# One of the seven products of a pair of score tiles, made as seven products of quarter size

## The chip, the cores and the metric

The kernel runs on one core of one Trainium2 chip. The metric is device time in microseconds (us) of that core, the median of several runs. Lower is better.

## The reference, cut to what matters

Two graph layers over 4096 nodes with 512 features each. Layer 0 adds `relu(adj @ signs)` to `x` and normalises. Layer 1 is masked attention, and the change lies in its scores `e = h @ h.T`:

```python
# layer 0
xw  = max(sign(x), 0) @ sign(weight).T
x   = layernorm(x + relu(adj @ xw))
# layer 1
h   = x @ edge_w                         # 4096 x 512, float32
e   = h @ h.T                            # 4096 x 4096 scores, float32
e   = where(adj > 0, e, -9e15)
att = softmax(x @ node_w, axis=0) * softmax(e, axis=1)
x   = layernorm(x + (adj * att) @ (x @ weight) + bias)
```

The scores are symmetric, so only one triangle of tiles is computed, and the mirrored tile is its transpose.

## The kernel before

`hT` holds `h` transposed: 128 partitions, four slices of the 512 features, 4096 nodes. The score matrix is cut into tiles of 512 x 512 (`W` = 512), numbered by row `A` and column `B`, 0 to 7. Single tiles are made by `Single` (line L706, a plain product). The others come in pairs: `Couple(A, B)` makes tile (A, B) and tile (A, B+1), 512 rows by 1024 columns, with Strassen's scheme in Winograd's form: the rows are halved (blocks `u` of 128 rows inside each half `q`), the features are halved, and the columns are halved, so that seven products of half size take the place of eight. `Couple.operands` builds the sums for this: four sums `t1` to `t4` of the column operand for each `B` (L747 to L750), and four sums `s1` to `s4` of the row operand for each couple (L764 to L767), all on VectorE (DVE).

`Couple.quad(q, between)` makes one half `q` of a couple. `multiply(bank, m)` (L779) issues product number `m`: two matmuls of 128 x 128 weights and 512 moving columns, because half the features are two slices. An fp32 matmul shows as two records in the trace, so one such product is four records. The order and what follows each product is:

- product 0 into bank `y`, copied to `c11` by ScalarE (ACT, L803); product 1 into bank `x`, added to `c11` by DVE (L806);
- product 5 added into `y`, copied to `c12` (L810); product 4 into `z`;
- product 6 added into `y`, copied to `c22` (L816), then `z` added to it by DVE (L817);
- product 3 added into `y`, copied to `c21` (L821); product 2 added into `z`, and `z` added to `c12` (L824). Then both strips of rows, (c11, c12) and (c21, c22), are complete: `written(0)` and `written(1)`.

A strip is half of a `lent` buffer (`free_h` holds 14 such halves). For every complete strip three kinds of work are queued: DVE masks it and takes the row minimum (L629, L630), after which ACT takes the exponential (L639); TensorE (PE) transposes it for the mirrored tiles (L668), and ACT copies the transposes out (L669), which then get their own L630 and L639; the GpSimd queue (POOL) stores it (L796), and the mirrored tiles too (L682). The masks come in by SyncE's queue (SP, L611, L614).

There are twelve couples in three runs: four for B = 4, six for B = 6, two for B = 2, with Single tiles before, between and after them. In a run, the quads of neighbouring couples are interleaved by hand as generators (`next(first)`, `next(second)`, `next(rest_)`), and `between()` counts the steps (`tick`) and lets queued work out. A scheduler then places the instructions of PE, DVE and ACT in this stage by when it expects them to be ready; each engine runs its list in order. From the aggregation stage on (L955 and after) the order is fixed by hand.

Of the kernel before, what the change touches and what calls it, by code (L numbers as in the profile page):

```python
# [11 lines left out]
F32 = mybir.dt.float32  # L12
# [6 lines left out]
P = 128  # L19
# [10 lines left out]
def kernel(  # L30
# [13 lines left out]
    nc = tc.nc  # L44
# [3 lines left out]
    W = 512  # L48
# [12 lines left out]
    ps_mm = ctx.enter_context(tc.tile_pool(name="ps_mm", bufs=6, space=bass.MemoryType.PSUM))  # L61
# [97 lines left out]
    with (  # L159
# [281 lines left out]
        l11, l12 = we_s[:, :HK, :HD], we_s[:, HK:, :HD]  # L441
        l21, l22 = we_s[:, :HK, HD:], we_s[:, HK:, HD:]
        s4, s1, s2, s3 = (lops[:, n] for n in range(4))
# [88 lines left out]
    free_h = deque(h for t in lent for h in t[1:])  # L532
# [195 lines left out]
                    stats.append((at_once, 0, store))  # L728

    class Couple:  # L730
        right = {}
        made = [0]

        def __init__(self, A, B):
# [6 lines left out]
        def operands(self):  # L741
            A, B, h = self.A, self.B, KD // 2
            if B not in Couple.right:
                r11, r12 = (hT[:, :h, ts(c, W)] for c in (B, B + 1))
                r21, r22 = (hT[:, h:, ts(c, W)] for c in (B, B + 1))
                t1, t2, t3, t4 = (lopp.tile([P, h, W], F32, name="right", tag="lop") for _ in range(4))
                nc.vector.tensor_sub(t1, r12, r11)  # L747
                nc.vector.tensor_sub(t2, r22, t1)
                nc.vector.tensor_sub(t3, r22, r12)
                nc.vector.tensor_sub(t4, r21, t2)  # L750
                Couple.right[B] = r11, r21, r22, t4, t1, t2, t3
            low, high = (hT[:, f : f + h, ts(A, W)].rearrange("p k (q u w) -> p k q u w", u=2, w=P) for f in (0, h))
            l11, l21 = (low[:, :, :, u, :] for u in range(2))
            l12, l22 = (high[:, :, :, u, :] for u in range(2))
            Couple.made[0] += 1
            self.sums = None
            if Couple.made[0] % 2:
                s2, s1, s3, s4 = (rows.tile([P, h, 2, P], F32, name="left", tag="rows") for _ in range(4))
            else:
                self.sums = Uses(1)  # L760
                s2, s1, s3, s4 = (
                    self.sums.buf[:, n, :].rearrange("p (k q w) -> p k q w", k=h, w=P) for n in range(4)
                )
            nc.vector.tensor_add(s1, l21, l22)  # L764
            nc.vector.tensor_sub(s2, s1, l11)
            nc.vector.tensor_sub(s3, l11, l21)
            nc.vector.tensor_sub(s4, l12, s2)  # L767
            self.left = l11, l12, s4, l22, s1, s2, s3

        def quad(self, q, between):  # L770

            left, right = self.left, Couple.right[self.B]
            x, y, z = (ps_mm.tile([P, W], F32, name="seven", tag="mm") for _ in range(3))
            strips = [Uses(4, free_h) for _ in range(2)]
            (c11, c12), (c21, c22) = ((s.buf[:, 0, :], s.buf[:, 1, :]) for s in strips)

            def multiply(ps, m, first=False):
                for k in range(KD // 2):
                    nc.tensor.matmul(  # L779
                        ps,  # L780
                        left[m][:, k, q, :],
                        right[m][:, k, :],
                        start=(first and k == 0),
                        stop=(k == KD // 2 - 1),
                        skip_group_check=not first,
                    )

            def written(u):
                s, i = strips[u], 2 * q + u
                here = self.here[i]  # L790
                stats.append((here.ready, 1, lambda: here.row(i, s, s.buf.rearrange("p c w -> p (c w)"))))
                for n, m in enumerate(self.mirrors):
                    turns.append((now[0] + 2, lambda m=m, n=n: m.turn(s, s.buf[:, n, :], i)))

                def store():
                    nc.gpsimd.dma_start(s_d[self.A][self.B // 2][:, i, :, :], s.buf)  # L796
                    s.used()

                stats.append((at_once, 0, store))


            multiply(y, 0, True)
            nc.scalar.copy(c11, y)  # L803
            between()
            multiply(x, 1, True)
            nc.vector.tensor_add(c11, c11, x)  # L806
            between()
            yield
            multiply(y, 5)
            nc.scalar.copy(c12, y)  # L810
            between()
            multiply(z, 4, True)
            between()
            yield
            multiply(y, 6)
            nc.scalar.copy(c22, y)  # L816
            nc.vector.tensor_add(c22, c22, z)  # L817
            between()
            yield
            multiply(y, 3)  # L820
            nc.scalar.copy(c21, y)  # L821
            between()
            multiply(z, 2)
            nc.vector.tensor_add(c12, c12, z)  # L824
            written(0)
            written(1)
            between()
            yield
# [52 lines left out]
    def spend(engine, cost, ready=0.0):  # L881
        clock[engine] = max(clock[engine], ready) + cost
        return clock[engine]
# [47 lines left out]
    class Aggregate:  # L931
# [143 lines left out]
        def second(self, m):  # L1075

            h, w = BG // 2, W // 2
            r = self.right(m)
            (r11, r12), (r21, r22) = [[r[:, k : k + h, c : c + w] for c in (0, w)] for k in (0, h)]
            t2, t3, t4 = (extra[0][:, n, :].rearrange("p (b w) -> p b w", w=w) for n in range(3))  # L1080
            self.halves = r11, r21, r22, t4, r12, t2, t3
            for o, a, b in ((t3, r22, r12), (r12, r12, r11), (t2, r22, r12), (t4, r21, t2)):
                nc.vector.tensor_sub(o, a, b)
                spend("dve", 0.69)
                yield
# [40 lines left out]
    written = deque()  # L1126
# [97 lines left out]
    inner, inner_next = deque(), deque()  # L1224
# [196 lines left out]
    def couples(B, *As):  # L1421
        return [Couple(A, B) for A in As]

    runs = [Single(2, 2), Single(2, 3), couples(4, 2, 3, 0, 1)]
    runs += [Single(4, 4), Single(4, 5), couples(6, 2, 3, 0, 1, 4, 5)]
    runs += [Single(3, 3), couples(2, 0, 1)]
    tail = len(runs)
    runs += [Single(0, 0), Single(0, 1), Single(1, 1), Single(6, 6), Single(6, 7), Single(7, 7), Single(5, 5)]
    masks = deque(r for u in runs for c in (u if isinstance(u, list) else [u]) for r in c.masks)
# [2 lines left out]
    def between():  # L1432
        tick()
        soon[0] = max(1, 2 - sum(m.t is not None for m in final))
        while masks and len(free_h) > 2 and masks_h[0] < 8 and masks[0].unit <= unit[0] + 1:
            masks.popleft().load()
        for _ in range(2):
            if closing[0] and len(early_) > 1 and (len(early_) > 10 or now[0] % 2) and early_[0][0]():
                early_.popleft()[1]()
            if len(early_) < 10:  # L1440
                break
# [10 lines left out]
    for n, u in enumerate(runs):  # L1452
        unit[0] = n
        closing[0] = n >= tail
        if isinstance(u, Single):
            final = []
            u.main(between)
            for later in runs[n + 1 : n + 3]:
                if isinstance(later, list) and later[0].left is None:
                    later[0].operands()  # L1460
            continue
        final = u[-1].mirrors
        quads = [[c.quad(q, between) for q in range(2)] for c in u]
        for k, c in enumerate(u):
            first, second = quads[k]
            rest_ = quads[k - 1][1] if k else None
            next(first)
            if rest_:
                next(rest_)
            next(first)  # L1470
            if rest_:
                next(rest_)
                if u[k - 1].sums:
                    u[k - 1].sums.used()
            next(first)
            next(second)
            if k + 1 < len(u):
                u[k + 1].operands()
            next(first)
            next(second)  # L1480
        next(rest_ := quads[-1][1])
        next(rest_)
        if u[-1].sums:
            u[-1].sums.used()
# [13 lines left out]
    r11, r12, r21, r22 = (w1_s[:, k : k + 2, c : c + HD] for k in (0, 2) for c in (0, HD))  # L1498
    t2, t3, t4 = (take(free_e).rearrange("p (k o) -> p k o", o=HD) for _ in range(3))
# [5 lines left out]
    with tc.manual_schedule(engines=order_):  # L1505
        for n, u in enumerate(blocks):
# [5 lines left out]
            first = deque()  # L1512
# [60 lines left out]
            if u.r == HG - 1 and nxt:  # L1573
                todo.extend(Todo(lambda g=u.g, n=n: join(g, n, nc.vector)) for n in range(7))
                second, other = (Finish(u.g, half) for half in (1, 0))
# [49 lines left out]
```

## Time and profile before

| | us |
|---|---|
| median of 3 runs | 1921.03 (1920.61 to 1921.36) |
| the profiled execution's own time | 1922.03 |
| its span in the trace | 1920.3 |
| PE busy (share of the span) | 1904.1 (99%) |
| DVE busy | 1437.1 (75%) |
| ACT busy | 1023.4 (53%) |
| POOL busy | 310.6 (16%) |
| the couples run in the trace from | 629 to 995, with Single tiles at 740 to 765 and 930 to 940 |

In the groups of the profile a row reads: line, engine, operation, what it writes and reads, shapes and count, then the busy time, the mean duration of one instruction in ns, and the idle time of the engine just ahead of them with what ended it. The durations of matmuls overlap, so that the distance between two starts is shorter than the duration. PEld is the load of weights, which runs beside the matmuls.

### The profile page before, as it was taken

The page shows a single profiled execution, that of the slowest core. Times are in us where ns is not written, and L with a number is a line of the kernel's source. Part 1 is how long each engine was busy: PE and PEld are TensorE (multiplying, and loading weights), DVE is VectorE, ACT ScalarE, POOL GpSimd, SP SyncE. Part 2 cuts the span into 40 slices and gives each one's busy share as a digit, 9 for nine tenths or more (in the row PEclk, how much of TensorE's full clock was granted, in tenths as well). Part 3 has the DMA queues.
Part 4 walks back from the last instruction along what each step waited for, and adds up shares of the span by engine and source line. Part 5 has one row for each costly group of instructions (what it writes and reads, how often), then busy time and mean ns, then how long its engine had stood idle before and what let it go on. Part 6 is the DMA issues. An engine that isn't in the chain of part 4 may idle for free.

```text
span 1920.3 us, 20431 instructions
## 1 busy us (share of the span) xinstructions
PE 1904.1 (99%) x6816; PEld 1220.4 (64%) x6816; DVE 1437.1 (75%) x2113; ACT 1023.4 (53%) x1647; POOL 310.6 (16%) x449
## 2 busy tenths in 40 slices
PE   8999999999999999999999999999999999999998
PEld 6888888888644445444555556666666666656646
DVE  6777677776875467576754877898879988898947
ACT  5433333333212468566767666656676567657731
POOL 0123132231421011111110111111111111110100
PEclk9999999999999999999999999999999999999999
DMA  8889898898585478477874888787777877787731
GB/s 307 288 327 354 318 333 322 326 356 317 177 300 199 153 280 321 178 255 276 306 282 156 309 291 299 285 292 287 266 282 279 298 277 276 264 308 250 285 117 55
DMA packets 143913, 520.93 MB, mean 271 GB/s; under 512 B 15040, under 2 KB 15040, under 8 KB 136128
## 3 DMA queue, kind: packets, MB, share of 16 engines
q1 hardware_dynamic: 64368, 235.43, 35.9%
q0 software_dynamic: 67632, 248.54, 34.2%
q10 hardware_dynamic: 11808, 35.66, 5.0%
q8 instruction: 54, 0.88, 0.2%
q14 instruction: 51, 0.42, 0.1%
HBM read 397.93 MB, written 121.63 MB: 271 GB/s over the span
## 4 chain that ended last, share of the span: by engine, by line
PE 89%; DVE 6%; ACT 2%; DMA 1%; issue 1%; ACTq 0%; DVEq 0%
PE bank L1186 33%; PE seven L779 14%; PE acc L424 11%; PE acc L423 11%; PE pe L706 5%; PE seven L101 5%; PE po L1336 4%; PE pt L668 2%; DMA lent<-in_adj_t_dram 1%; DVE slot L955 1%; PE pt L383 1%; PE acc L236 1%; PE acc L235 1%; PE pw L213 1%; PE bank L1336 0%
## 5 line engine op out<-in xcount | busy, mean ns | idle before, releaser
L1186 PE MATMUL bank<-lent,lop 128*128 128x256 f32 (+1 forms) x1496 | 483.0, 473 | 0.1
L1186 PEld LDWEIGHTS bank<-lent,lop 128*128 128x128 f32 x1496 | 283.8, 190 | 166.9 <-issue 140.1
L423 PE MATMUL acc<-xw,hi 128*128 128x512 f32 x960 | 376.4, 392 | 0.0
L424 PE MATMUL acc<-xw,lo 128*128 128x512 f32 x960 | 374.2, 390 | 0.0
L1186 PE MATMUL bank<-slot,lop 128*128 128x512 f32 (+1 forms) x800 | 286.6, 503 | 2.6 <-DMA lop<-lop_d 1.3
L413 ACT CAST hi<-at 128x1024 fp32r<-128x1024 f32 x120 | 126.5, 1054 | 203.7 <-PE acc L423 151.0
L1186 PEld LDWEIGHTS bank<-slot,lop 128*128 128x128 f32 x800 | 151.4, 190 | 117.6 <-issue 102.5
L1197 ACT COPY over<-bank 128x512 f32<-128x512 f32 x200 | 116.2, 586 | 199.8 <-PE bank L1186 195.9
L424 PEld LDWEIGHTS acc<-xw,lo 128*128 128x128 f32 x960 | 180.3, 188 | 37.1 <-DVE lo L415 0.3
L423 PEld LDWEIGHTS acc<-xw,hi 128*128 128x128 f32 x960 | 180.2, 188 | 36.7
L415 DVE TENSOR_TENSOR lo<-at,hi 128x1024 fp32r<-128x1024 f32 x120 | 147.9, 1232 | 66.8 <-ACT hi L413 66.4
L706 PE MATMUL pe<-hT 128*128 128x512 f32 (+3 forms) x384 | 132.1, 486 | 0.0
L639 ACT ACTIVATE line<-line,nmax_c 128x512 f32<-128x512 f32 x160 | 114.8, 725 | 22.6 <-DVE nmax_c L630 22.3
L630 DVE CUSTOM_DVE_ANT_0 line<-lent,slot 128x512 f32<-128x512 bf16 x140 | 90.7, 689 | 47.6 <-ACT slot L716 26.7
L1348 DVE SCALAR_TENSOR_TENSOR xb<-po,f,xb 128x256 f32<-128x256 f32 x84 | 40.2, 480 | 74.7 <-PE po L1336 70.5
L706 PEld LDWEIGHTS pe<-hT 128*128 128x128 f32 x384 | 64.6, 191 | 41.4 <-issue 33.8
L779 PE MATMUL seven<-hT 128*128 128x512 f32 x192 | 89.8, 593 | 0.0
L955 DVE CUSTOM_DVE_ANT_1 lent<-lent,line 128x2048 f32<-128x2048 f32 x39 | 88.7, 2283 | 0.0
L1159 ACT COPY bank<-over 128x512 f32<-128x512 f32 x144 | 86.7, 603 | 0.0
L668 PEld LDWEIGHTS pt<-ident,lent 128*128 128x128 f32 x418 | 52.3, 141 | 52.1 <-issue 38.5
L669 ACT COPY slot<-pt 128x512 f32<-128x512 f32 (+3 forms) x123 | 68.5, 560 | 23.2 <-PE pt L668 23.2
L958 ACT ACTIVATE lent<-lent 128x2048 f32<-128x2048 f32 x39 | 74.9, 1920 | 8.4 <-DVE lent L955 8.2
(270 smaller groups left out, 2947.0 us busy)
## 6 DMA issues: line engine op xcount, KB each, us to landing
lop<-lop_d SPq DMA_DIRECT2D x154, 512.0 KB, 4.7
at<-in_adj_t_dram SPq DMA_DIRECT2D x60, 1024.0 KB, 6.7
slot<-in_adj_t_dram POOLq DMA_DIRECT2D x39, 1024.0 KB, 8.0
lent<-s_d POOLq DMA_DIRECT2D x38, 1024.0 KB, 7.8
s_d<-slot POOLq DMA_DIRECT2D x30, 1024.0 KB, 7.0
lent<-in_adj_t_dram POOLq DMA_DIRECT2D x25, 1024.0 KB, 7.7
lent<-in_adj_dram SPq DMA_DIRECT2D x48, 512.0 KB, 5.0
s_d<-lent POOLq DMA_DIRECT2D x48, 512.0 KB, 4.1
```

The source lines that it names most:

```text
L101: nc.tensor.matmul(banks[bank][q], lop(m, q)[k], rop(m)[k], start=(first and k == 0), stop=(k == K - 1), skip_group_check=not first,)
L413: nc.scalar.copy(hi, aq)
L415: nc.vector.tensor_sub(lo, aq, hi.bitcast(F32))
L423: nc.tensor.matmul(acc, hi[:, c, :], xw[:, kb, :], start=(kb == 0), stop=False)
L424: nc.tensor.matmul(acc, lo[:, c, :], xw[:, kb, :], start=False, stop=(kb == NB - 1))
L639: nc.scalar.activation(line, line, AF.Exp, bias=nmax_c[:, b, c : c + 1], scale=-1.0, accum_out=sum_c[:, b, c : c + 1])
L668: nc.tensor.transpose(pt[:, j, :], src[:, ts(j, P)], ident)
L706: nc.tensor.matmul(pe[:, lo * P :], hT[:, k, ts(A * BG + i, P)], hT[:, k, (B * BG + lo) * P : (B + 1) * W], start=(k == 0), stop=(k == KD ...
L779: nc.tensor.matmul(ps, left[m][:, k, q, :], right[m][:, k, :], start=(first and k == 0), stop=(k == KD // 2 - 1), skip_group_check=not first,)
L955: pinned[0](nc.vector._custom_dve(TENSOR_ADD_SAT, out=q, in0=q, in1=m, s0=0.0, s1=-HUGE))
L1186: nc.tensor.matmul(ps, lop[:, k, :], rop[:, k, :], start=start, stop=(k == K - 1), skip_group_check=True)
L1197: nc.scalar.copy(self.to(), self.bank[:, : self.w])
```

## The change

Product 1 of both quads of a couple (features' second half of the upper blocks by the first column tile, second half of the features) is no longer issued by `quad`. Seen over both quads it is one product of 256 rows by 512 columns over 256 features, and it is cut once more by the same scheme: rows by quad, columns into two halves of 256 (`w`), features into two slices of 128. Seven products of one matmul each, with 256 moving columns, take the place of four matmuls with 512.

- `second_right` builds four sums of 128 x 256 for each `B`; `second_left` builds four sums of 128 x 128 for each couple. Each set lies in one half of a `lent` buffer, taken from `free_h`; the first is kept while its `B` lasts, the second until the couple is done.
- `second` issues the seven small products. They are named here by bank and number: u0, v1, u5, z4, u6, z2, u3, in this order. `u` is the left half of a bank `x`, `v` and `z` are the halves of a bank `y`. DVE adds the results to `c11` of the two quads: u to the left half after u0, to the right half after u5, z to the right half of the second quad's strip after z4, u to the same after u6, the whole bank `y` to the first quad's strip after z2, and u to the left half of the second quad's strip after u3. Products 5, 6 and 3 go on top of what stands in `u`, and 2 on top of `z`, once DVE has read it.
- A quad uses two banks instead of three. Its generator has one more stop, `c11` is complete later, and the first strip of the first quad is released from inside `second`. The twelve small stops are interleaved with the quads.

```diff
+                Couple.inner_right[B] = self.second_right(r21)
...
+            self.inner_left = self.second_left(l12)
+            self.rows11, self.written = [None] * 2, [None] * 2
+
+        def second_right(self, r):
+
+            w = W // 2
+            (r11, r12), (r21, r22) = ((r[:, k, :w], r[:, k, w:]) for k in range(2))
+            keep = Uses(sum(c.B == self.B for c in every), free_h)
+            t1, t2, t3, t4 = (keep.buf[:, n // 2, ts(n % 2, w)] for n in range(4))
+            nc.vector.tensor_sub(t1, r12, r11)
+            nc.vector.tensor_sub(t2, r22, t1)
+            nc.vector.tensor_sub(t3, r22, r12)
+            nc.vector.tensor_sub(t4, r21, t2)
+            return (r11, r21, r22, t4, t1, t2, t3), keep
+
+        def second_left(self, l):
+
+            (l11, l12), (l21, l22) = ([l[:, k, q, :] for k in range(2)] for q in range(2))
+            self.inner_sums = Uses(1, free_h)
+            s1, s2, s3, s4 = (self.inner_sums.buf[:, 0, ts(n, P)] for n in range(4))
+            nc.vector.tensor_add(s1, l21, l22)
+            nc.vector.tensor_sub(s2, s1, l11)
+            nc.vector.tensor_sub(s3, l11, l21)
+            nc.vector.tensor_sub(s4, l12, s2)
+            return l11, l12, s4, l22, s1, s2, s3
+
+        def second(self, between):
+
+            left, (right, keep) = self.inner_left, Couple.inner_right[self.B]
+            w = W // 2
+            c11, c12 = (self.rows11[0][:, c] for c in (slice(w), slice(w, W)))
+            x, y = (ps_mm.tile([P, W], F32, name="inner", tag="mm") for _ in range(2))
+            u, v, z = x[:, :w], y[:, :w], y[:, w:]
+
+            def multiply(ps, m, first=False):
+                nc.tensor.matmul(ps, left[m], right[m], start=first, stop=True, skip_group_check=not first)
+
+            multiply(u, 0, True)
+            nc.vector.tensor_add(c11, c11, u)
+            yield
+            multiply(v, 1, True)
+            multiply(u, 5)
+            nc.vector.tensor_add(c12, c12, u)
+            between()
+            yield
+            c21, c22 = (self.rows11[1][:, c] for c in (slice(w), slice(w, W)))
+            multiply(z, 4)
+            nc.vector.tensor_add(c22, c22, z)
+            yield
+            multiply(u, 6)
+            nc.vector.tensor_add(c22, c22, u)
+            multiply(z, 2)
+            nc.vector.tensor_add(self.rows11[0], self.rows11[0], y)
+            self.written[0]()
+            between()
+            yield
+            multiply(u, 3)
+            nc.vector.tensor_add(c21, c21, u)
+            self.inner_sums.used()
+            keep.used()
+            yield
 
         def quad(self, q, between):
 
-            x, y, z = (ps_mm.tile([P, W], F32, name="seven", tag="mm") for _ in range(3))
+            y, z = (ps_mm.tile([P, W], F32, name="seven", tag="mm") for _ in range(2))
...
+            self.rows11[q] = c11
...
             multiply(y, 0, True)
             nc.scalar.copy(c11, y)
             between()
-            multiply(x, 1, True)
-            nc.vector.tensor_add(c11, c11, x)
-            between()
+            self.written[q] = lambda: written(0)
             yield
             multiply(y, 5)
             nc.scalar.copy(c12, y)
             between()
+            if q:
+                yield
             multiply(z, 4, True)
...
+            if not q:
+                yield
             multiply(z, 2)
             nc.vector.tensor_add(c12, c12, z)
-            written(0)
+            if q:
+                written(0)
             written(1)
...
             next(first)
+            inner_ = inners[k]
+            next(inner_)
             next(second)
             if k + 1 < len(u):
                 u[k + 1].operands()
+            next(inner_)
             next(first)
+            next(inner_)
+            next(first)
+            next(inner_)
+            next(second)
+            next(inner_)
             next(second)
```

More of the change, by code (lines that the diff above doesn't have):

```diff
@@ L730 @@
     class Couple:
-        right = {}
+        right, inner_right = {}, {}
         made = [0]
@@ L1426 @@
     runs += [Single(3, 3), couples(2, 0, 1)]
+    every = [c for u in runs if isinstance(u, list) for c in u]
     tail = len(runs)
@@ L1463 @@
         quads = [[c.quad(q, between) for q in range(2)] for c in u]
+        inners = [c.second(between) for c in u]
         for k, c in enumerate(u):
```

## The prediction

> **What bounds the kernel now.** I read the page's busy shares first, then the busy time in windows of one couple each, then the groups with shapes kept apart, then the chain of waits from 600 us on. The page says that PE is the bound everywhere:
>
> ```profile
> PE 1904.1 (99%) x6816; PEld 1220.4 (64%) x6816; DVE 1437.1 (75%) x2113; ACT 1023.4 (53%) x1647; POOL 310.6 (16%) x449
> ```
>
> The windows (PE, PEld, DVE, ACT, POOL busy, clock, DMA share, GB/s) say how near the next engine is, couple by couple. A couple takes about 27.5 us, all of it PE; DVE has 10 us to spare in an early couple and 4.5 us in the last one of a run, where the column sums of the next `B` (L747 to L750) are built too:
>
> ```profile
> 656.50:684.00 27.50, 27.50 (x89) 13.77 (x88) 15.15 (x32) 16.48 (x36) 3.61 (x6) 1.00 0.58 211
> 711.50:739.00 27.50, 27.50 (x89) 13.66 (x89) 23.00 (x45) 20.38 (x43) 3.63 (x6) 1.00 0.80 283
> ```
>
> ```profile
> 904.60:932.00 27.40, 27.40 (x91) 13.75 (x91) 22.93 (x43) 18.72 (x40) 4.43 (x8) 1.00 0.84 303
> 939.70:967.00 27.30, 26.57 (x78) 12.48 (x77) 12.11 (x28) 17.47 (x43) 2.01 (x4) 1.00 0.69 257
> ```
>
> The groups give the durations:
>
> ```profile
> L1186 PE MATMUL bank<-lent,lop 128*128 128x256 f32 x840 | 196.3, 379 | 0.1
> L779 PE MATMUL seven<-hT 128*128 128x512 f32 x192 | 89.8, 593 | 0.0
> L779 PEld LDWEIGHTS seven<-hT 128*128 128x128 f32 x192 | 33.4, 190 | 26.8 <-issue 26.8
> L1348 DVE SCALAR_TENSOR_TENSOR xb<-po,f,xb 128x256 f32<-128x256 f32 x84 | 40.2, 480 | 74.7 <-PE po L1336 70.5 <-DMA lop<-lop_d 4.1
> L806 DVE TENSOR_TENSOR lent<-lent,seven 128x512 f32<-128x512 f32 x24 | 16.5, 687 | 48.0 <-PE seven L779 28.9 <-issue 19.1
> L1243 DVE TENSOR_TENSOR slot<-slot 128x256 f32<-128x256 f32 x16 | 6.7, 422 | 0.3
> ```
>
> The chain (start, us, engine, line) holds what the busy share hides. Nearly all of it is PE, but from 908 to 948 us it leaves PE: 39 us of DVE and ACT work end in a PE stall of 0.72 us at the start of the B = 2 run.
>
> ```profile
> 899.86 8.60 PE seven L779 x20
> ...
> 908.49 0.69 DVE lent L824
> ...
> 937.17 1.24 ACT lent L639 x2
> ...
> 945.22 2.11 ACT line L639 x6
> 947.33 0.48 ACT lent L810
> ...
> 947.86 10.57 PE seven L779 x24
> ```
>
> **What the Trainium skill says.** "TensorE: Matmul & The Clock Gate", section LDWEIGHTS, puts a weight load at columns/1.2 ns, 107 ns for 128; here it is 190 ns. That still fits under a 256-column record. "VectorE: DVE Perf Modes", section on the TRN2 errata, gives an fp32 add (N+151)/0.96 ns: 691 at 512 (here 687), 424 at 256 (here 422). No 128-column add shows here; the page prices it at 291 ns (estimate). "PSUM — Partial Sum Buffer", section Engine vs sequencer instructions, says that the queues of VectorE and ScalarE are strictly in order; the stall at 947 agrees, since the copy of `c12` (L810) stood behind a row of L639 exponentials. "DMA: Bandwidth & Descriptors", section Anatomy of one DMA, gives 2.0 us plus bytes at 436 GB/s, 3.2 us for a 512 KB store (estimate); L796 took 3.6 us (770 to 900 us) and 5.5 us (650 to 735 us).
>
> **PE's own work.** In unbroken stretches of the chain a 512-column record starts every 0.429 us (28 in 12.02 us); four 256-column ones (L1336 at 1303.9 us) take 0.87, 0.217 each. Per couple 8 records of 0.429 go (3.43 us) and 14 of 0.217 come (3.04 us): 0.39 us less, times 12 couples, **-4.7 us**. The load of 190 ns hides under 217.
>
> **DVE's own work, per couple:** two adds of 687 ns go; five of 256 columns (422) and one of 512 (687) come, with four row sums of 128 columns (291): +2.6 us. Per `B` four column sums of 422: +1.7 us. In all +36 us, beside PE's work where the spare of 10 us covers it. ACT, POOL and SP get no new work: the same copies, exponentials, stores and loads, only later or earlier. Buffers: 14 halves now also hold one for each `B` and up to two for couples. Counting the code's steps, masks are still loaded at least 8 steps ahead of their use (a couple has 14, so 2 us each), 16 us against a landing of 4 to 5: taken at nothing, up to 3 us if it is wrong.
>
> **The new waits, in a middle couple.** I follow the built order of the changed kernel with the durations above, from the end of the previous quad's product 6 (t = 0). PE: four transposes to 0.43, u0 0.86, next quad's product 0 to 2.58, transposes 3.01, v1 3.44, u5 3.87, transposes, product 3 and transposes 6.45, z4 6.88, product 2 to 8.60, u6 9.03, z2 9.46, then transposes, product 5, transposes to 12.04, u3. DVE: `c22` add (after ACT's copy) 0.95 to 1.55, mask L629 to 2.15, add of u0 to 2.6; u5 loads its weights at 3.2, so 0.6 us to spare. Then L630 to 3.75, three row sums of the next couple to 4.6, add of u5 to 5.05, four L630 (held by ACT's copy until 5.65) to 8.15, add of z4 to 8.6; z2 loads at 8.8, 0.2 to spare. The adds of u6 and u3 have over 1 us. The three row sums stand ahead of the add of u5 and wait for the store of the buffer that they overwrite: issued at about -0.7, landed at 3 to 4.8 by the times above, so 0 to 0.7 us late. Behind that DVE wait stand the adds, L630 and thus ACT; PE waits for the add of z4. I take 0.1 us for each of nine couples, **+0.8 us** (0 to 6).
>
> **The ends of the B = 4 and B = 6 runs.** Here DVE must make L747, which waits for the last product 4 (14.2 on the clock above), then add u3, then L748, L749 and two or three row sums of the next run, and only then the `c22` add for which the last product 2 waits. B = 4: 14.4 + 1.15 + 0.4 + 1.15 + 0.6 + 0.6 + 1.15, so the `c22` add ends at 20.05; PE wants it at 19.0: **+1.0 us** (0 to 2). In the trace of before L817 ended at 737.18 and PE went on with product 2 at 738.2. B = 6 has one row sum more (1.65 us late), and its DVE chain leads into the stall at 947: it gets the adds (+2.2), second sums for B = 2 and for two couples, against two exponentials fewer ahead of the copy of `c12` in ACT's order. I put that copy 1.2 us later than before while PE wants it no later: a stall near 2 in place of 0.72, **+1.3 us** (0 to 4.5); the lateness is shared with that run's end, so it counts once.
>
> After the last couple the built order of PE and DVE is what it was, and PE carries the end, so what is won or lost passes through. Sum: -4.7 + 0.8 + 1.0 + 1.3 = **-1.6 us**: span 1920.3 to 1918.7, and with the 1.7 us around it 1922.0 to 1920.4; the median of before stands 1.0 below the profiled run, so **1919.4 us**.
>
> **Rivals.** (1) DVE keeps up everywhere: the whole 4.7 is won, less some tenths: 1916.5. For it: PE shows hardly a wait for DVE among couples now, and the walk finds slack at every small product. Against: 0.2 us is little, and the 908 to 948 chain. (2) DVE becomes the bound through the order in which it runs: if the add of z4 is on average more than 0.39 us late for z2, each couple loses what it won. At 0.9 us late, 12 couples give +10.8 against -4.7, and the run ends count in it: 1927.1, slower. For it: 2.6 us more DVE in a queue that already stops for ACT copies and would now stop for stores; against: DVE idles 10 us in most couples. (3) The change doesn't do what it says: two 256-column records cost more than one of 512 because weight loads show. At 0.19 + 0.05 us per record 14 of them take 3.36 us, PE saves 0.9 us in all and the stalls stay: 1923.2; the 0.87 us for four at 1303.9 speaks against.
>
> **How the numbers follow.** A measurement of this kernel can tell about 0.2% (3.8 us) from no change. Forecast (stalls of 0.9 to 8.5 us) 0.50; rival 1 0.24; rival 2 0.21; rival 3 0.05. Rival 1 lies beyond 0.2%, all the forecast's range (-3.8 to +3.8) within it with rival 3, and nearly all of rival 2 slower: faster 0.24, same 0.54, slower 0.22. The forecast's own range is 1917.2 to 1924.8. The range to 1915.8 takes in rival 1, and to 1925.0 the near part of rival 2; what is left out is its far part.
>
> **What would show it.** Right: 84 small products as 168 records, 0.217 us apart in a row; couples near 27.1 us; DVE over 25 us in the last couples of B = 4 and 6; PE waits for DVE of 1 to 2 us at those ends, a longer stall at the start of B = 2. Wrong: small records 0.24 us apart; PE waits for DVE at u5 or z2 in most couples (rival 2), or no PE wait anywhere (rival 1); PE waits on masks, which would mean that the buffers taken were not free.

## The result, and the profile after

| | median, us | ratio to the kernel before, 95% interval |
|---|---|---|
| kernel before (15 runs beside it) | 1921.50 | 1 |
| changed kernel (15 runs) | 1916.88 (1915.17 to 1918.34) | 0.9975, 0.9967 to 0.9983 |

The change makes the kernel 4.6 us faster, a quarter of a per cent. Run twice more beside other kernels it gave 1917.04 and 1916.84 us. The time lies in the range that was stated, but next to the first rival (1916.5), not on the forecast (1919.4), and outside the forecast's own range (1917.2 to 1924.8). So PE's own work was sized right, and nearly all of the 3.1 us of new stalls that the forecast set against it did not come.

The page of the changed kernel has fewer PE us with more records, and only 21.8 us more of DVE, not 36. In the chain the share of PE went from 89% to 93% and that of DVE from 6% to 3%: the other engines carry less of the end than before.

```profile
PE 1900.7 (99%) x6888; PEld 1234.3 (64%) x6888; DVE 1458.9 (76%) x2221; ACT 1024.2 (53%) x1647; POOL 309.6 (16%) x449
...
PE 93%; DVE 3%; DMA 1%; issue 1%; ACT 1%; ACTq 0%; POOL 0%; DVEq 0%; POOLq 0%
```

The windows (PE, PEld, DVE, ACT, POOL busy with instructions, clock, DMA share, GB/s) are read against those of before. A couple is 27.14 us long in the trace, where it was 27.55 (the first line below, from the trace of before), and PE is busy in all of it. The last two lines are the last couples of B = 4 and B = 6. DVE has 21.9 and 24.4 us there, for 23.0 and 22.9 before; the forecast had put it over 25. The new column sums of the next `B` begin behind these windows (743.81 and 932.39 us), and so does L750 of B = 4 (740.92).

```profile
844.77:872.32 27.55, 27.55 (x89) 13.77 (x89) 17.82 (x38) 18.83 (x40) 3.62 (x6) 1.00 0.75 263
```

```profile
652.57:679.71 27.14, 27.14 (x95) 14.91 (x95) 17.08 (x41) 17.90 (x39) 3.59 (x6) 1.00 0.53 196
...
840.16:867.30 27.14, 27.14 (x96) 14.90 (x95) 21.49 (x48) 19.13 (x41) 3.60 (x6) 1.00 0.72 263
```

```profile
709.80:737.00 27.20, 27.20 (x96) 14.96 (x95) 21.91 (x45) 17.84 (x38) 3.59 (x6) 1.00 0.81 292
902.50:929.60 27.10, 26.90 (x100) 14.93 (x99) 24.44 (x49) 17.90 (x38) 4.37 (x8) 1.00 0.84 311
```

The groups of the window 600 to 1000 us show the new operations. L805 is the matmul of the small products, L808 to L827 are their adds, L790 one of the four row sums, L779 one of the four column sums. The last number of a row is the idle time of the engine ahead of the group: it is nothing for the small products, and what stands in front of the adds is PE, on which they have to wait in any case. The 128-column sum, which no trace had shown, takes 286 ns; "VectorE: DVE Perf Modes" of the Trainium skill, section on the TRN2 errata, gives 291 by its formula (estimate).

```profile
L805 PE MATMUL inner<-lent,lent 128*128 128x256 f32 x66 | 19.6, 379 | 0.0
...
L822 DVE TENSOR_TENSOR lent<-lent,inner 128x512 f32<-128x512 f32 x12 | 8.2, 681 | 0.0
...
L817 DVE TENSOR_TENSOR lent<-lent,inner 128x256 f32<-128x256 f32 x12 | 5.0, 416 | 1.8 <-PE inner L805 1.8
...
L790 DVE TENSOR_TENSOR lent<-hT 128x128 f32<-128x128 f32 x12 | 3.4, 286 | 0.3 <-DMA s_d<-lent 0.3
...
L779 DVE TENSOR_TENSOR lent<-hT 128x256 f32<-128x256 f32 x3 | 1.3, 418 | 0.0
```

The waits of PE's weight loads from 600 to 1100 us (us in total, times, longest) answer the walk through a middle couple. A load is the first part of a product that meets a wait. No load of a small product waited more than 0.2 us for DVE, and the matmuls behind these loads show no wait at all. The only wait of size for DVE is that of a plain product for the `c22` add (now L880), 1.0 us at the longest, at the end of B = 6. ("issue" is no wait for another engine.)

```profile
PEld seven L842 <- issue: 93.0, 389, 0.2
...
PEld seven L842 <- ACT lent L866: 2.7, 3, 1.6
PEld inner L805 <- DVE nmax_c L630: 2.2, 9, 0.2
PEld seven L842 <- DVE lent L880: 1.5, 3, 1.0
...
PEld inner L805 <- DVE lent L817: 0.5, 2, 0.2
```

The chain from 900 to 950 us can be put beside that of before. It leaves PE at the end of B = 6 as it did then, for sums and stores, and comes back twice: at 924.35 behind the `c22` add, and at 939.86 behind the copy of `c11` (L866). Ahead of the `c22` add it now holds a store of 1024 KB (`s_d<-slot`), for which DVE stood before it wrote a sum that had been there before the change (L765).

```profile
910.81 8.69 DMA s_d<-slot
...
922.56 1.14 DVE right L749
923.69 0.61 DVE lent L880
924.35 1.98 PE seven L842 x4
...
938.62 0.71 ACT line L639 x2
939.33 0.48 ACT lent L866
939.86 2.84 PE seven L842 x6
```

**Where the 4.6 us come from.** I compare the start of the same instruction in both traces:

| place | before | after | difference | couples so far x 0.41 |
|---|---|---|---|---|
| first row of 256 columns of the Single tile behind B = 4 | 746.67 | 745.01 | -1.66 | 1.64 |
| the same behind B = 6 | 936.77 | 933.08 | -3.69 | 4.10 |
| start of the Single tile behind B = 2 | 996.58 | 992.08 | -4.50 | 4.92 |
| first product of the aggregation | 1075.12 | 1070.62 | -4.50 | |

Twelve couples win 4.9 us, the end of B = 6 gives 0.4 back, and the rest passes through whole. The two profiled spans differ by 0.9 more (5.4 us), but that arises after 1070 us, in a stage which the change does not touch. Each span is of a single execution, and the medians differ by 4.6 us.

### The profile page after: what moved, and what is told of

Read it like the earlier page. It is cut to its first block, busy times and chain, and to the rows that moved or that the text cites. A ratio compares the mean times of both kernels' runs of the same rounds, so it can differ in the third digit from the quotient of the medians.

```text
span 1914.9 us, 20669 instructions
## 1 busy us (share of the span) xinstructions
PE 1900.7 (99%) x6888; PEld 1234.3 (64%) x6888; DVE 1458.9 (76%) x2221; ACT 1024.2 (53%) x1647; POOL 309.6 (16%) x449
## 4 chain that ended last, share of the span: by engine, by line
PE 93%; DVE 3%; DMA 1%; issue 1%; ACT 1%; ACTq 0%; POOL 0%; DVEq 0%; POOLq 0%
PE bank L1252 36%; PE seven L842 12%; PE acc L424 11%; PE acc L423 11%; PE pe L706 6%; PE seven L101 5%; PE po L1402 4%; PE pt L668 3%; PE inner L805 2%; PE pt L383 1%; PE acc L236 1%; PE acc L235 1%; PE pw L213 1%; PE bank L1402 0%; DMA lop<-lop_d 0%
## 5 line engine op out<-in xcount | busy, mean ns | idle before, releaser
L630 DVE CUSTOM_DVE_ANT_0 line<-lent,slot 128x512 f32<-128x512 bf16 x140 | 90.2, 687 | 54.6 <-ACT slot L669 28.6
L1027 ACT ACTIVATE slot<-slot 128x2048 f32<-128x2048 f32 x37 | 71.1, 1922 | 7.7 <-DMA slot<-in_adj_t_dram 7.7
```

What stands on the lines that cost most here:

```text
L630: nc.vector.tensor_tensor_reduce(line, mask, src, -1.0, HUGE, ALU.add, ALU.min, accum_out=nmax_c[:, b, c : c + 1])
```

## The experiments

All times are medians, each with the kernel before on the same chip.

| kernel | us | before, us | ratio, 95% interval |
|---|---|---|---|
| v1_twice | 1921.17 | 1921.33 | 1.0000, 0.9992 to 1.0008 |
| in_a_row | 1947.63 | 1921.33 | 1.0131, 1.0116 to 1.0147 |
| dve_plus_6 | 1917.11 | 1921.33 | 0.9979, 0.9971 to 0.9986 |
| dve_plus_18 | 1930.17 | 1921.35 | 1.0046, 1.0033 to 1.0060 |
| sums_only | 1925.17 | 1921.33 | 1.0018, 1.0011 to 1.0024 |
| sums_kept | 1921.18 | 1921.30 | 1.0000, 0.9992 to 1.0008 |
| only_b6 | 1920.26 | 1921.30 | 0.9994, 0.9987 to 1.0000 |
| only_b6_kept | 1918.39 | 1921.35 | 0.9985, 0.9979 to 0.9992 |
| two_products | 1915.64 | 1921.30 | 0.9969, 0.9958 to 0.9981 |
| two_products_5 | 1915.47 | 1921.10 | 0.9968, 0.9956 to 0.9981 |
| after_again, after_5 | 1917.04, 1916.84 | 1921.30, 1921.10 | 0.9976 (0.9966 to 0.9987), 0.9976 (0.9968 to 0.9985) |

### Is it PE's own work? One small product more

```diff
             multiply(v, 1, True)
+            multiply(v, 1, True)
```

> The changed kernel with the small product v1 issued twice in each couple; the second overwrites the first, so the computation is unchanged. PE-bound theory (the whole gain is PE's own work and no other engine sets the pace): one small product is two records of 0.217 us, 12 couples give 12 x 0.43 = +5.2 us on the changed kernel's 1916.9, so about 1922.1 us, ratio to the kernel before 1.0003. Rival (PE waits for DVE in each couple and has time to spare): the extra product falls into a wait and costs under 2 us, so 1917 to 1919. Rival that small records cost more in place than in a row (0.24 us): +5.8, 1922.7; the distances between starts in the trace tell this from 5.2.

The median rose by 4.3 us on the changed kernel. In the trace a couple of the B = 4 run is 27.57 us long (680.72 to 708.29), 0.43 more than 27.14, and so in every couple looked at: PE has no slack there into which a product could fall, and two small records cost 2 x 0.217 in place as they do in a row. The Single tile behind B = 2 comes 4.7 us later than in the changed kernel (4.84, less the 0.16 by which this trace runs late at 606 us). Most of the 0.5 us that are missing from 5.2 come back at the end of B = 6, where PE arrives later and no longer stands for the `c22` add (0.36 us in the changed kernel). That is how a stage bound by PE looks, with one place in it that is not.

### Are the new waits real? The small products in a row

(In this kernel the products of a couple are pinned to the order in which they are written.)

```diff
-            next(inner_)
             next(second)
...
-            next(inner_)
             next(first)
-            next(inner_)
             next(first)
-            next(inner_)
+            for _ in range(5):
+                next(inner_)
             next(second)
-            next(inner_)
             next(second)
```

> The changed kernel with the products of a couple pinned in program order and the small ones put in a row: u0, v1, u5, z4, u6, z2, u3 ahead of the second quad's product 4 or so, with only transposes free to go between. Theory that the waits on DVE's adds are real and that the interleaving hides them: u5, u6, z2 and u3 each wait for an add that has at most one product of 0.43 us beside it; an add of 0.42 us with the hand-over before and after it leaves about 0.5 us of stall each, 2 us per couple, 12 couples +24 us: about 1940 us (1930 to 1955, more where the add stands behind a mask row of 1.1 us). Rival (DVE keeps up anyhow, interleaving doesn't matter): within 3 us of 1916.9.

It cost 30.7 us, 2.6 per couple against the 2 expected. One couple in the order of time shows where it goes: three of its small products stand behind an add.

```profile
845.77 0.70 PE L805 MATMUL inner<-lent,lent 128*128 128x256 f32 x2 [0.59 <-DVE lent L813]
...
847.24 0.70 PE L805 MATMUL inner<-hT,lent 128*128 128x256 f32 x2 [0.78 <-DVE lent L818]
848.19 0.70 PE L805 MATMUL inner<-lent,hT 128*128 128x256 f32 x2 [0.25 <-DVE lent L821]
```

The waits of PE from 600 to 1100 us name the adds (L813 is the add of u5, L818 that of z4, L821 that of u6, L809 that of u0):

```profile
PE inner L805 <- DVE lent L813: 5.1, 9, 0.7
PE inner L805 <- DVE lent L818: 4.1, 6, 0.8
PE inner L805 <- DVE lent L821: 2.1, 7, 0.4
...
PE inner L805 <- DVE lent L809: 0.6, 3, 0.3
```

These are 11.9 us of the matmuls; the weight loads in front of them waited 26.8 us for the same four adds, and the two overlap. So the seven products do depend on DVE one after another, and it is the plain products between them that hide it. In this pinned order, losing the interleaving costs more than six times what the change wins. Two things are mixed into the 30.7 us. The plain products are pinned too, and no run pins them alone, though in the trace nearly all late starts of PE are at small products. And in two stretches of this trace (876.0 to 884.7 and 940 to 946 us) the granted clock was 0.61 and 0.72 in place of 1.00; 512-column records started 0.85 us apart there, which makes some 4 us in all (estimate from these distances).

### How near is DVE to its limit? Operations put ahead of the add of z4

(dve_plus_18 has 18 in place of 6.)

```diff
             multiply(z, 4)
+            for _ in range(6):
+                nc.vector.tensor_sub(self.inner_sums.buf[:, 1, :w], right[1], z)
             nc.vector.tensor_add(c22, c22, z)
```

> The changed kernel with six more DVE operations in each couple, each reading z after z4 into an unused part of a buffer, all ahead of the add of z4 (256 columns, 0.42 us each, starting about 0.34 us apart): 2.0 to 2.5 us more of DVE per couple, 30 us in all. z2 may load only when the last of them has read z. PE's order is free, and in this kernel it is built with z2 further back, behind one more plain product. Theory that DVE has spare time in most couples and that the order built from expected times gives the adds room: middle couples stay near 27.1 us; the last couples of B = 4 and B = 6 and the start of B = 2 lose up to 2.5 us each: 1918 to 1924 us. Rival (DVE's order is at its limit with 0.2 us to spare): 1.8 us later in each couple, 12 x 1.8 = +22, so 1939 us.

> As dve_plus_6 with eighteen more DVE operations in each couple in place of six: 18 x 0.34 = 6.1 us more DVE work per couple, so about 22.6 us of 27.1 in a middle couple and 31 us in the last couples of B = 4 and B = 6. Theory that DVE's busy time, and not its order, is what would end the gain: middle couples stay within 0.5 us of 27.14, the last couples and the starts of runs lose about 4 us each, 1923 to 1932 us in all. Rival (the order, as soon as six operations are too many for one place): 2 us or more in each couple, 1940 us or more.

Six operations raised DVE's busy time by 24.1 us (1483.0) and the median by 0.2 us. This speaks against the second rival, which needed a lateness of only 0.39 us per couple to turn the gain into a loss: 2.0 us of work went ahead of the add that the walk had found 0.2 us short of its limit, and a couple in the B = 6 run still took 27.18 us.

```profile
840.99:868.17 27.18, 27.18 (x95) 14.81 (x95) 23.84 (x55) 18.75 (x41) 3.60 (x6) 1.00 0.72 267
```

It did not fit in by slack alone. PE's order was built anew with the six in it. In the changed kernel one plain product stands between z4 and z2 in every couple; here there are three in nine of the twelve (not two, as the expectation had it), so z2 starts 6.9 us after z4 and not 2.6: two plain products more (four matmuls of 2 x 0.429) and two groups of transposes. Even so the room is used up. The loads of small products now wait for the add of z4 (L819), and z2 starts up to 0.25 us late in four couples; shorter stalls at the end of B = 6 and the start of B = 2 make up for it.

```profile
PEld inner L805 <- DVE lent L819: 6.7, 11, 0.8
```

A walk along a fixed order can't see that PE's order moves.

Eighteen cost 13.3 us on the changed kernel. Both expectations were off in part: the total lies in the first theory's span, but middle couples did not stay within 0.5 us of 27.14.

```profile
647.13:674.80 27.67, 27.55 (x96) 14.94 (x95) 25.70 (x64) 15.86 (x33) 3.80 (x6) 1.00 0.50 178
838.72:868.27 29.55, 28.26 (x95) 14.64 (x95) 27.60 (x66) 17.62 (x39) 3.72 (x6) 1.00 0.71 259
897.01:927.20 30.19, 28.28 (x96) 14.63 (x95) 25.44 (x61) 18.43 (x41) 3.70 (x6) 1.00 0.74 261
```

With 25.7 us of DVE a couple lost 0.5 us, with 27.6 it lost 2.4, but the last couple of B = 6 lost about 3 with 25.4. So the free ride ends once DVE is asked for about as much time as a couple has, but DVE's busy time alone does not say how much is lost: the order counts as well, and it was built anew here too (z2 starts 15.5 us or more after z4). No run parts the two. My expectation had added 6.1 to the 16.5 us of an early couple; a couple of B = 6 has 21.5 to begin with.

### Are sums and buffers free? The kernel before with the sums, used by nothing

```diff
                 Couple.right[B] = r11, r21, r22, t4, t1, t2, t3
+                Couple.inner_right[B] = self.second_right(r21)
...
             self.left = l11, l12, s4, l22, s1, s2, s3
+            self.inner_left = self.second_left(l12)
```

> The kernel before, with the sums of the change (four of 256 columns for each B, four of 128 for each couple) built by DVE and their buffers held for as long as a couple lasts, but with product 1 still made as two plain products; the sums are used by nothing. DVE gets about 12 x 4 x 0.28 + 12 x 0.42 = 18 us of busy time. Theory that sums and buffers are covered by PE: 1921.5 us as before, within 1 us. Rival that buffers or DVE's order cost something which the change then wins back: 1923 us or more, and PE waits for DVE or for masks (SP) in the couples.

Neither: it is slower, by 3.8 us in the median, with runs from 1921.0 to 1927.9; the traced one is the slowest of them. The timeline names the place (start, us, engine, operation, and in brackets the idle time before it with its releaser). L782 is the first of the four column sums, and DVE stood idle in front of it for 3.36 and 3.04 us, at the starts of the B = 6 and B = 2 runs:

```profile
749.10 0.43 DVE L782 TENSOR_TENSOR lent<-hT 128x256 f32<-128x256 f32 x1 [3.36 <-PE pt L668]
...
940.75 0.42 DVE L782 TENSOR_TENSOR lent<-hT 128x256 f32<-128x256 f32 x1 [3.04 <-DMA s_d<-lent]
```

The second wait is put down to the store of the half that the sums overwrite; the first to PE's transposes out of it (several were waited for, and the one that the profile saw last is named). Behind DVE stand the mask rows (L630), behind these ACT's exponentials, and behind a run of exponentials in ACT's order the copy of `c11` (L870) for which PE waits. The waits of PE from 600 to 1100 us:

```profile
PE pt L668 <- ACT slot L716: 2.1, 2, 1.7
PE seven L846 <- ACT lent L870: 2.0, 2, 1.1
```

This is the wait that the prediction had named for the row sums of middle couples, at another place. To tell it from the cost of DVE's work, the sums of 256 columns were given one half for good:

```diff
-            keep = Uses(sum(c.B == self.B for c in every), free_h)
+            if not Couple.inner_right:
+                Couple.kept = Uses(len(every), free_h)
+            keep = Couple.kept
```

> As sums_only (the kernel before with the sums built and used by nothing), but the four sums of 256 columns go each time into one and the same half buffer, taken once and kept to the end of the couples, so that they never overwrite a half whose store may still be on its way. DVE does the same work and as many halves are held during the couples. Theory that the 3.8 us of sums_only came from DVE standing 3.4 and 3.0 us in front of the first of these sums, at the starts of the B = 6 and B = 2 runs, until a store had landed: these two waits go, and with them the stalls, 1921.5 us (1920.5 to 1922.5). Rival (DVE's 18 us of added work, or the smaller number of free halves, costs the 3.8 us): 1925 us as in sums_only.

Back at 1921.18 us, with the same amount of work done: DVE is busy for 1449.7 us here and for 1450.2 in sums_only (1437.1 before). The first column sum is L784 now, and nothing stands in front of it:

```profile
L784 DVE TENSOR_TENSOR lent<-hT 128x256 f32<-128x256 f32 x3 | 1.2, 415 | 0.0
```

This run alone does not part the wait from the work, since it moved the work as well: with one half and no reader, all twelve column sums were made at 608 to 617 us, ahead of the first couple. The changed kernel tells more. There the column sums of B = 6 and B = 2 are made at the starts of the runs (743.81 to 749.03 us and 932.39 to 937.61), with nothing in front of the first (L779, shown above), and PE stands no longer at these starts than before. So DVE's work for the sums is free at that place too, and what costs is the wait. In this order the half that they get has been read for the last time, by a store or by PE, before they come. A wait of this kind need not cost either. In the middle of the B = 6 run of the changed kernel DVE stood 3.7 us for a store, in front of a sum that the kernel before has too, and PE lost nothing:

```profile
DVE slot L765 <- DMA s_d<-slot: 4.4, 2, 3.7
```

The other of the two is the one at the end of that run. The prediction took buffers at nothing, from 0 to 3 us; that was right for this order, and a kernel that differs in little from it pays 3.8.

### Does each couple win? The change in B = 6 alone

```diff
+            self.split = B == 6
```

(With `split` off, a couple takes the code of the kernel before.)

> The change made in the six couples of B = 6 alone; the six of B = 4 and B = 2 keep product 1 as two plain products. PE-bound theory: 6 x 0.41 = 2.5 us less than the kernel before, minus 0.4 at the end of the run: 1919.3 us, half of the whole gain; couples of B = 6 27.14 us long, those of B = 4 27.55. Rival (the gain comes from one place, such as the start of the B = 2 run or a stall that the new order removes, not from each couple): 1921.5 or 1917 us.

> As only_b6 (the change in the six couples of B = 6 alone), but the half buffer for the four sums of 256 columns is taken once ahead of all couples, so that no store can still be reading it. In the profile of only_b6 DVE stood 3.1 us in front of the first of these sums and PE lost about 2.3 us at the start of the B = 6 run. Theory that each couple wins 0.41 us and only_b6 lost most of it in that wait: the wait goes, 1919.0 us (1918.3 to 1919.8), ratio 0.9988. Rival (half of the couples win less than half of the gain for another reason): 1920.3 us as in only_b6.

only_b6 won 1.0 us of the 2.1 expected, and its runs spread from 1917.3 to 1922.8. Its couples of B = 6 are 27.13 us long, as they should be, but the groups show DVE 3.1 us in front of L782 again, for a store, at the start of this run, and PE loses about 2.3 us there. With a half taken ahead of all couples this wait goes (and the first column sum with it, to 611 us), and the gain is 3.0 us, for 2.3 expected (1.5 to 3.0): in the trace the first row of 256 columns behind B = 2 starts at 999.55 us for 1002.36 before. Six couples give 2.5 us of the 2.8; the rest is a stall at the start of B = 2 that is shorter by more than the end of B = 6 takes back. The rival (a gain from one place) falls: half of the couples bring half of the 4.9 us, provided that the sums do not run into a store.

### A version that beats both: product 2 in the same way

Product 2 goes to `c12` alone, as product 1 goes to `c11` alone. Here nine couples, all but the last of each run, make it as seven small products too, in the second half of the couple (`more()` issues small products of the couple before).

```diff
-            multiply(z, 2)
+            if not self.split2:
+                multiply(z, 2)
             nc.vector.tensor_add(c12, c12, z)
...
             next(first)
+            more()
             if rest_:
                 next(rest_)
```

> The changed kernel with product 2 (s4 by the second half of the second column tile, which goes to c12 alone) made in the same way in the nine couples that are not the last of their run: seven more small products for each, with four sums of 256 columns for each B, four of 128 for each couple and six more adds on DVE; c12 is complete about 9 us later. Theory that PE's work is what counts while DVE has spare time (six more DVE operations per couple cost 0.2 us in all): 9 x 0.41 = 3.7 us less than the changed kernel, 1913.2 us, up to 2 us more where the starts of runs or the buffers held longer cost something. Rival (with 4 us more DVE work per couple, and strips held longer, DVE or the free halves become the bound): 1917 us or more.

> two_products once more, beside the changed kernel on one chip, since 1915.6 against 1917.0 us with six and eight runs does not tell the two apart. If its gain over the changed kernel is what its trace shows up to the aggregation stage (1.2 us), 1915.7 us; if the trace's loss later on is in every run, 1916.8 us; the gain from PE's own work alone would be 3.5 us, 1913.4 us.

The changed kernel ran beside each of the two:

> The changed kernel itself, beside the other three on one chip: 1916.9 us, 4.6 us less than the kernel before.

> The changed kernel itself beside two_products_5, as the yardstick for it: 1916.9 us, 4.6 us less than the kernel before.

1915.64 and 1915.47 us, 1.4 us below the changed kernel beside it both times, where PE's own work alone would have given 3.5. At the start of the aggregation stage its trace is 1.2 us ahead of the changed kernel's (DVE's first row there at 1056.37 for 1057.66, less the 0.12 by which it is early at 606 us). The other 2.3 us went where the second rival had looked for them: DVE is up to 1490.7 us, and PE waits for its adds. The first line below is a wait of the matmuls, the second, of weight loads, stands for several that are shorter (both from 600 to 1100 us). The third is a couple that lost 0.3 us in front of z2, with DVE busy for 21.0 us of 26.8: eight row sums in a row, where the changed kernel has four, run ahead of the adds (825.78 to 827.40 us).

```profile
PE pt L668 <- DVE lent L901: 0.9, 1, 0.9
```

```profile
PEld inner L813 <- DVE lent L825: 2.0, 6, 0.6
```

```profile
803.34:830.12 26.78, 26.77 (x99) 15.91 (x99) 21.02 (x52) 18.47 (x40) 3.31 (x7) 1.00 0.76 264
```

Against the kernel before it is faster by 0.31% (0.19 to 0.44 over both intervals). The intervals of the two against the kernel before overlap. Side by side on one chip they do not: the five runs of two_products_5 (1914.69 to 1915.65) all lie below the thirteen of the changed kernel (1915.74 to 1918.24). That it is faster is shown there; the size, 1.4 us, is less sure.

## Why the prediction was right or wrong, point by point

- **PE's own work, -4.7 us: right.** Measured -0.41 us per couple for -0.39 worked out, so -4.9. The spacing of 0.217 us for 256 columns, taken from four records of another stage, holds in place (v1_twice), and the load of 190 ns stays hidden. The third rival is out.
- **DVE's own work, +36 us: too much.** Its busy time rose by 21.8 us. The step added durations, and the durations in the trace do add up to 35 us more; but back to back, the next instruction of DVE starts before the last has ended, and busy time counts the overlap once. Starts lie 0.34 us apart for 256 columns (858.12 to 858.46), not 0.42, and 0.20 for 128 (938.14 to 938.34), not 0.29. With 0.60, 0.34 and 0.20 the same count gives 27 us (estimate from these distances); the rest is that other instructions of DVE follow each other more closely now. The conclusion, that it lies beside PE's work, stands (sums_kept, dve_plus_6).
- **Waits in a middle couple, +0.8 us: nothing.** In the couple that begins at 840 us (t = 0 at 850.30) the add of z4 started at 858.12 and ended at about 8.2 on the walk's clock, for 8.6; z2 was issued at 859.37. Three L630 stood ahead of it there, not four, and the row sums waited 0.3 us for a store in the whole window, not up to 0.7 in a couple. The mechanism exists (in_a_row), with more room than the walk gave it.
- **End of B = 4, +1.0 us: nothing, and here a step failed.** The walk let L747 wait for the last product 4, until t = 14.2. In the trace (t = 0 at 716.98) L747 ran at 729.72, t = 12.7, while product 4 was under way (729.50 to 731.22), and it was L748 that started behind product 4, at 731.42:

```profile
729.72 1.22 DVE L747 TENSOR_TENSOR right<-hT 128x1024 f32<-128x1024 f32 x1
...
730.86 0.41 DVE L827 TENSOR_TENSOR lent<-lent,inner 128x256 f32<-128x256 f32 x1
...
731.42 1.23 DVE L748 TENSOR_TENSOR right<-hT,right 128x1024 f32<-128x1024 f32 x1
```

  The new column sums can't be written each to the place of the old one of its name, then: the times fit a buffer that goes to whoever comes next once product 5 has read it last. That is inferred from the times, and the buffers' addresses were not looked at. The `c22` add ended at t = 18.7 for 20.05, and PE came for it at 19.4 for 19.0.
- **End of B = 6 and start of B = 2, +1.3 us: +0.4.** L749 and the `c22` add kept product 2 from 924.00 to 924.35, 0.36 us for 1.65. That it is so little has the same reason. That there is any, the prediction did not have: by the chain above DVE stood for the store in front of L765, and L748, L749 and the `c22` add followed without a gap:

```profile
919.52 0.69 DVE L765 TENSOR_TENSOR slot<-hT 128x512 f32<-128x512 f32 x1 [0.65 <-DMA s_d<-slot]
```

  The stall at the start of B = 2 did not grow to 2 us: PE stood from 938.93 to 939.86, 0.93 us, and had stood from 946.91 to 947.86, 0.95 us, before. Only its name changed, from the copy of `c12` to that of `c11`.
- **Buffers and masks at nothing: right for this order.** No wait of PE on masks, and none of the new sums waits for a store for more than 0.3 us. sums_only and only_b6 show how close it was.
- **The choice among the cases: this is what was wrong.** Rival 1 (1916.5, chance 0.24) is what happened. For the forecast three small lateness terms were added that all rested on the same walk, and each erred to the same side: durations in place of spacings, and the wait of L747 at the later of two places. As they shared their error they were no three reasons. That the number still fell into the stated range is owed to the rival, for whose sake the range went down to 1915.8, and not to the three terms. The waits of before already spoke for rival 1: from 604 to 1010 us no wait of PE for DVE was longer than 0.2 us. The two groups with the largest totals:

```profile
PEld pt L668 <- DVE nmax_c L630: 1.2, 5, 0.2
PEld pt L668 <- DVE lent L817: 1.0, 4, 0.2
```

What was to show it, then: the 168 small records at 0.217 us and the couples near 27.1 us are there; DVE over 25 us in the last couples, PE waits of 1 to 2 us at the run ends and a longer stall at B = 2 are not.

## What to carry to other kernels

Where PE is busy for the whole of a stage, what a change takes from PE's own records comes out of the time nearly one to one, as long as the next engine has time to spare and dependent small products lie apart with other products between them. Its busy share alone does not tell how much it may take on: DVE at 23.8 us of a couple of 27.2 cost next to nothing (dve_plus_6), at 21.0 of 26.8 it cost 0.3 us (two_products), where more of its work stood right ahead of an add for which PE waits. Walk a fixed order with the distances between starts and not with durations, and treat several lateness terms from one walk as one. A buffer taken for something new is free only if its last reader, a store above all, is done by then: look at the idle time in front of its first write, since it depends on the order and can cost nearly as much as the change wins (3.8 of 4.6 us).

## What the runs showed of the hardware that was not expected

- DVE starts its next instruction ahead of the end of the last: 0.60 us between starts for 512 columns of 0.68, 0.34 for 256 of 0.42, 0.20 for 128 of 0.285.
- A store of a half (512 KB) takes 4.1 us from issue to landing in the page of before, 4.4 in that of sums_only and 6.7 in that of the changed kernel (medians of 48), where "DMA: Bandwidth & Descriptors" of the Trainium skill, section Anatomy of one DMA, gives 3.2 (estimate). The prediction had 3.6 to 5.5 from two stretches of the trace. Why the same stores take longer in the changed kernel is not shown.
- The granted clock fell to 0.61 and 0.72 for some microseconds in the trace of in_a_row, and 512-column records were then 0.85 us apart, not 0.429. What set it off is not shown.
